# Gathers that add, replaced by gathers into work tiles and separate adds

## The chip, the cores and the metric

The kernel runs on one core of a Trainium2 chip. The metric is the time of one execution on the device in microseconds (us); lower is better. The engines in the profile are PE (TensorE, matrix products; PEld is its weight load), DVE (VectorE), ACT (ScalarE), POOL (GpSimd) and SP (SyncE, which here only issues DMAs). POOL also issues the DMAs whose rows are picked by a list of indices (DMA_INDIRECT). Each engine runs its own instructions strictly in order; semaphores make one engine or DMA wait for another.

## The reference

Sixteen sequences of 256 tokens, 128 values each, in float32, pass two layers. Between the steps every token is normalised.

```
x = x + 0.5 * moe(layernorm(x))            # "a"
x = x + attention(layernorm(x))            # 16 heads of 8, differential, causal
x = x + 0.5 * moe(layernorm(x))            # "b", the same weights
x = x + 0.5 * quant_ffn(layernorm(x))      # "qa"
x = x + linear_attention(layernorm(x))     # "l", a scan over the tokens
x = x + 0.5 * quant_ffn(layernorm(x))      # "qb"
```

The part that the change touches is the mixture of experts, which runs twice. A shared expert serves every token; of eight further experts each token takes the two with the highest router score, weighted by the softmax of these two scores:

```
logits = xf @ router_w.T + experts_bias
rw, sel = jax.lax.top_k(logits, 2)
rw = softmax(rw)
cw = (one_hot(sel, 8) * rw[..., None]).sum(axis=1)
eo = silu(einsum('td,edh->teh', xf, w1)) * einsum('td,edh->teh', xf, w3)
out = einsum('te,teh,ehd->td', cw, eo, w2) + shared_out
```

## The kernel before

The 4096 tokens lie in SBUF all the time, as eight blocks `xs[k]` of 128 partitions x 4 tiles (`NT`) x 128 values; a block is two sequences. Every step updates its block in place.

A mixture is done for a group of one or two blocks (`GROUPS`, line 35): "a" for [0], [1], [2, 3], [4, 5], [6, 7], "b" for [0, 1], [2, 3], [4, 5], [6], [7]. The first, a0, runs every expert over all its tokens. The other nine route:

- `route` (line 550) normalises the blocks, scores the tokens and picks two experts for each; `send` (line 642) computes for each token the two rows (`pos`) that it gets in a table sorted by expert.
- `scatter` (line 695) copies the tokens into that table in DRAM (`slots_x`) by indirect DMAs of 128 rows from POOL, line 714, two in flight at a time.
- `experts` fetches the table in tiles of 128 rows (`xg`), runs each through the weights of its one expert (`wst`, loaded by SP; products `pgu` and `poy` on PE, the gate `hr` on ACT, DVE and sometimes POOL), scales the rows by the token's weight and writes them to a second table in DRAM (`slots_y`), issued by ACT.
- `collect` (line 939) waits for all experts of the group and for the shared expert and then starts one `gather` for each block (line 952).
- `gather` brings each token its two rows. For both of the two choices (`i`) and each of the four tiles (`t`) an indirect DMA from POOL (line 966) reads 128 rows of `slots_y` and adds them to `x[:, t, :]` as it writes. That is eight DMAs a block, and 15 blocks make 120. The second choice's DMA of a tile must come after the first has landed, since both add to the same bytes.

The first reader of the new tokens is `stats` (line 505): for each tile one `bn_stats` and one `bn_aggr` on DVE (lines 512, 513), then on POOL a small addition and a power (lines 516, 500), then on DVE `nm` (line 520). After "a" the attention (`project`, `maxima`, `weights`, `values`, `output`) follows, after "b" `quant` (line 1503), `linear` and `quant` again. The linear stage (`linear_f`, line 1689) runs eight rounds for each block: it loads `kv` (256 KB, line 1693, by SP), multiplies it by the keys (line 1698), scans (line 1701, DVE), multiplies by the queries (line 1705) and adds to a product on PE.

Nothing of this is a fixed loop. Each step is a Python generator that yields what it needs: engines it may run on with a cost, buffers and events. `Order.run` plays all of them against a book of free times for engines and buffers and issues the instructions one by one; so it decides the order on every engine. Two things of that matter here. `sb2` (line 392) offers an elementwise step to DVE or POOL, and the one that would finish first in the book takes it (DVE is charged 1 us extra). And `best_order` (line 306) makes 60 trial plans, each after the first with the ranks of five kinds of task moved at random, draws these from the sorted list of task names, and keeps the plan whose book ends first.

Work tiles are taken by tag from a fixed number of buffers and given back with `done`. Tag `w5` has seven buffers of 128x512 and serves the gates of the shared expert, the quantised layer's `thq`, and the linear stage's `kv`, `state`, `vT` and `thl`, and early on some weights that are unpacked.

Of the kernel before, what the change touches and what calls it, by code (L numbers as in the profile page):

```python
# [15 lines left out]
ALU = mybir.AluOpType  # L16
# [3 lines left out]
P = 128  # L20
B, S, D = 16, 256, 128
NBLK = 8
NT = 4
# [16 lines left out]
def slot_tiles(nt):  # L40


    return (2 * nt * P + E * (P - 1)) // P
# [207 lines left out]
def by_rows(index):  # L251
    return index if isinstance(index, Dry) else bass.IndirectOffsetOnAxis(ap=index, axis=0)
# [37 lines left out]
def e_pool(n, k=1):  # L290
    return k * (0.25 + n * 0.0029)
# [36 lines left out]
def program(order, nc, tc, const, small, work, ps, t_in, out):  # L328
# [40 lines left out]
    def W(tag, shape, name, dtype=F32):  # L369
        return (tag, name, shape, dtype)  # L370
# [13 lines left out]
    def hold(*want):  # L384

        return Op([("", 0.0)], want)
# [5 lines left out]
    def sb2(n, *want, need=None):  # L392

        return Op([("DVE", 0.16 + n * 0.0014), ("POOL", e_pool(n))], want, need)
# [10 lines left out]
    def on(g):  # L405
        return nc.vector if g.eng == "DVE" else nc.gpsimd
# [532 lines left out]
    def collect(w, j, rank):  # L939

        r = R[w, j]
        if (w, j) in DENSE:
            yield Wait(*(f"dense {w}{j}.{e}" for e in range(E)))
        else:
            yield Wait(f"experts {w}{j}", *(f"shared {w}{j}.{n}" for n in range(r["n"])))
            names = [f"gather {w}{j}.{n}" for n in range(r["n"])]
            for n, name in enumerate(names):
                order.add(name, gather(w, j, n), rank, order.events[f"experts {w}{j}"])
            yield Wait(*names)
        order.release(r["index"], 0.0)  # L950

    def gather(w, j, n):

        r = R[w, j]
        nt = NT * r["n"]
        sy = slots_y[w, j % 2][0 : slot_tiles(nt) * P]
        x = xs[GROUPS[w][j][n]]
        if n:
            yield Wait(f"gathering {w}{j}.{n - 1}")
        landed = {}  # L960
        for i in range(2):
            for t in range(NT):
                need = (landed[t],) if i else (order.events[f"experts {w}{j}"],)
                g = yield Op([("POOL", 1.6)], kb=1, need=need)
                a = i * nt + n * NT + t
                nc.gpsimd.indirect_dma_start(  # L966
                    x[:, t, :], None, sy, by_rows(r["pos"][:, a : a + 1]),
                    compute_op=ALU.add,
                )
                landed[t] = g.t  # L970
        order.mark(f"gathering {w}{j}.{n}", 0.0)
        order.mark(f"gathered {w}{j}.{n}", max(landed.values()))


    wqkv, bqkv = ctile([P, 640], "wqkv"), ctile([P, 640], "bqkv")
# [747 lines left out]
    def mixture(w, j, rank, *names):  # L1723
        n = f"{w}{j}"
        order.add(f"route {n}", after(route(w, j, rank), "ident", *names), rank)
        for i, k in enumerate(GROUPS[w][j]):
            order.add(f"shared {n}.{i}", shared(w, j, i, k), rank)
        if (w, j) in DENSE:
            for e in range(E):
                order.add(f"dense {n}.{e}", dense_expert(w, j, e), rank + 0.01 * e)  # L1730
        else:
            order.add(f"experts {n}", experts(w, j, rank), rank)
        order.add(f"collect {n}", after(collect(w, j, rank), f"route {n}"), rank)
# [43 lines left out]
    for j, blocks in enumerate(GROUPS["b"]):  # L1777
        rank = 10.0 - j
# [73 lines left out]
```

## Time and profile before

Three runs took 1311.86, 1313.22 and 1316.47 us; the median is 1313.22 us.

| what | value |
|---|---|
| profiled execution | 1316.87 us |
| its span, first to last instruction | 1315.2 us |
| mean granted clock of TensorE in it | 0.965 |
| DMA traffic | 149.68 MB, 114 GB/s over the span |
| POOL, other large groups: line 500, `rr` (16 powers of 128x32) | 87.9 us |
| line 500, `rs` (40 powers of 128x4) | 46.0 us |
| line 1705 on POOL (33) and on DVE (31) | 47.3 and 28.1 us |
| line 1698 on POOL (28) and on DVE (36) | 42.4 and 27.3 us |
| line 1577 on POOL (12) and on DVE (4) | 16.7 and 3.2 us |
| issue to landing, median: line 714 | 2.9 us |
| issue to landing, median: line 966 | 3.7 us |

The page of the profile gives for each engine its busy time and share of the span. A second part shows the span in 40 equal slices, one digit each (9 is 90% busy or more); PEclk is the clock that the throttle granted TensorE. Groups of instructions are shown as line, engine, operation, output<-inputs and count, then busy time in us and the mean of one in ns, then the idle time of that engine just before them and what ended most of it. "issue" there is time in which the engine waited for nothing that the profile shows. The chain of waits follows the work that ended last back from the last instruction.

The runs of line 966 start at 164, 303, 433, 563, 696, 909, 1033, 1111 and 1169 us.

### The profile page before, as it was taken

Reading aid. Unit: us, or ns where it says so; the run is one execution under the profiler, and the core shown is the slowest. Engines: PE = TensorE matmul, PEld = TensorE weight load, DVE = VectorE, ACT = ScalarE, POOL = GpSimd, SP = SyncE. Lnnn points to the kernel's source line nnn. Section 1 sums busy time; section 2 is a strip of 40 time slices with the busy share of each in tenths; the row PEclk is TensorE's granted clock in tenths of the full one; section 3 lists DMA queues with packets and bytes.
Section 4 is the critical chain, followed back from the end, with each engine's and each line's share of the span. In section 5 each row is a group of like instructions: output and inputs, shape, how many; then the busy total and the mean of one; then the engine's idle time right before and its main releaser. Section 6 shows DMA issues by size and latency. Waiting matters only on the chain. (4 is left out here: it accounts for less than half of the span.)

```text
span 1315.2 us, 32976 instructions
## 1 busy us (share of the span) xinstructions
PE 1175.2 (89%) x12480; PEld 853.7 (65%) x12480; DVE 897.6 (68%) x2059; ACT 655.5 (50%) x1163; POOL 821.7 (62%) x972
## 2 busy tenths in 40 slices
PE   6797889999899979998987799999999869898888
PEld 3465666676576667766754577767567657675566
DVE  5465667776678655594776568768748757587993
ACT  2153456554555544645633475664564524544424
POOL 4213546738862882384458735477867788779874
PEclk9898999999999989998998799999999989998989
DMA  4675563525344335445222333314445766642331
GB/s 127 147 194 132 140 161 87 143 67 125 88 128 128 52 86 159 127 105 125 69 82 27 88 90 104 88 52 110 100 129 161 206 158 169 169 127 77 93 100 33
DMA packets 213006, 149.68 MB, mean 114 GB/s; under 512 B 18544, under 2 KB 200944, under 8 KB 212848
## 3 DMA queue, kind: packets, MB, share of 16 engines
q1 hardware_dynamic: 155376, 113.70, 31.0%
q0 software_dynamic: 21120, 15.81, 6.8%
q10 hardware_dynamic: 36352, 18.07, 4.8%
q8 instruction: 99, 1.62, 0.5%
q14 instruction: 59, 0.48, 0.1%
HBM read 117.32 MB, written 30.19 MB: 112 GB/s over the span
## 5 line engine op out<-in xcount | busy, mean ns | idle before, releaser
L409 PE MATMUL pgu<-xTg,wst 128*128 128x128 f32 x1464 | 218.5, 285 | 10.9 <-DMA wst<-in_w_dram 6.1
L409 PEld LDWEIGHTS pgu<-xTg,wst 128*128 128x128 f32 x1464 | 188.7, 195 | 37.8 <-issue 19.2
L1264 DVE TENSOR_REDUCE qpad<-scores 128x8 f32<-128x2048 f32 x64 | 146.4, 2288 | 40.2 <-PE scores L413 39.7
L1323 ACT ACTIVATE ex<-scores 128x2048 f32<-128x2048 f32 x64 | 120.2, 1878 | 85.6 <-PE scores L413 85.5
L409 PE MATMUL poy<-wst,hr 128*128 128x128 f32 x732 | 117.3, 287 | 20.2 <-POOL hr L754 9.1
L413 PE MATMUL scores<-qm,kT 32*128 32x256 f32 (+1 forms) x2048 | 114.1, 349 | 16.1 <-DVE qpad L1264 9.8
L413 PE MATMUL scores<-kT,qT 32*128 32x512 f32 (+1 forms) x1024 | 113.4, 536 | 14.0 <-ACT ex L1323 4.9
L409 PEld LDWEIGHTS poy<-wst,hr 128*128 128x128 f32 x732 | 98.5, 196 | 36.8 <-DVE hr L737 11.7
L966 POOL DMA_INDIRECT x<-slots_yb,pos x64 | 106.5, 1664 | 17.5 <-issue 15.8
L928 ACT ACTIVATE y<-poy,xg 128x128 f32<-128x128 f32 x162 | 59.2, 368 | 98.0 <-PE poy L409 93.1
L413 PEld LDWEIGHTS scores<-qm,kT 32*128 32x128 f32 x2048 | 79.6, 189 | 41.5 <-DVE qpad L1264 16.2
L413 PE MATMUL pav<-ex,vaug 128*32 128x512 f32 (+1 forms) x1024 | 98.4, 503 | 2.3 <-ACT ex L1323 2.2
L966 POOL DMA_INDIRECT x<-slots_ya,pos x56 | 87.6, 1565 | 17.2 <-issue 14.2
L500 POOL TENSOR_TENSOR rr<-ss,mhalf 128x32 f32<-128x32 f32 x16 | 87.9, 5492 | 16.5 <-DVE ss L1401 16.4
L714 POOL DMA_INDIRECT slots_xa<-xng,pos x56 | 56.0, 1001 | 61.3 <-DMA slots_xa<-xng,pos 30.4
L413 PEld LDWEIGHTS pol<-owr,state 128*128 128x128 f32 x512 | 68.5, 207 | 37.9 <-POOL state L1705 18.9
L413 PE MATMUL pol<-owr,state 128*128 128x128 f32 x512 | 74.8, 295 | 20.3 <-POOL state L1705 13.9
L516 POOL TENSOR_SCALAR rs<-mv 128x4 f32<-128x4 f32 (+1 forms) x56 | 19.8, 353 | 117.2 <-DVE mv L513 116.4
L1701 DVE TENSOR_TENSOR_SCAN state<-lam,kv 128x512 f32<-128x512 f32 x64 | 90.3, 1423 | 1.4 <-POOL kv L1698 1.1
L413 PEld LDWEIGHTS <-shift 32*128 32x128 bf16 x3072 | 59.2, 95 | 48.3 <-issue 37.5
L714 POOL DMA_INDIRECT slots_xb<-xng,pos x64 | 67.6, 1057 | 35.4 <-DMA slots_xb<-xng,pos 13.5
L1247 DVE TENSOR_REDUCE qpad<-scores 128x16 f32<-128x2048 f32 x32 | 73.2, 2289 | 22.7 <-PE scores L413 22.4
(250 smaller groups left out, 2651.8 us busy)
## 6 DMA issues: line engine op xcount, KB each, us to landing
wst<-in_w_dram SPq DMA_DIRECT2D x573, 128.0 KB
kv<-values_l SPq DMA_DIRECT2D x64, 256.0 KB
xg<-slots_xb SPq DMA_DIRECT2D x21, 258.0 KB
slots_yb<-y ACTq DMA_DIRECT2D x21, 256.0 KB
xg<-slots_xa SPq DMA_DIRECT2D x18, 258.0 KB
slots_ya<-y ACTq DMA_DIRECT2D x18, 256.0 KB
slots_xa<-zero ACTq DMA_DIRECT2D x10, 258.0 KB
slots_xb<-zero ACTq DMA_DIRECT2D x10, 258.0 KB
```

The costliest lines, as they stand in the source:

```text
L409: nc.tensor.matmul(dst, lhsT, rhs, start=start, stop=stop)
L413: nc.tensor.matmul(dst, lhsT, rhs, start=start, stop=stop, skip_group_check=True)
L500: nc.gpsimd.tensor_tensor(dst, src, mhalf[:, :n], ALU.pow)
L516: nc.gpsimd.tensor_scalar(rs, mv[:, 0:nt, 1], LN_EPS, None, ALU.add)
L714: ins = nc.gpsimd.indirect_dma_start(sx, by_rows(r["pos"][:, i * nt + t : i * nt + t + 1]), xn[:, t, :], None,)
L928: nc.scalar.activation(y[:, i, :], po[:, 0:D], AF.Copy, scale=xg[:, i, D:SW])
L966: nc.gpsimd.indirect_dma_start(x[:, t, :], None, sy, by_rows(r["pos"][:, a : a + 1]), compute_op=ALU.add,)
L1247: nc.vector.tensor_reduce(qp[:, 0, T0 : T0 + 2, :, :, HD].rearrange("p t m g -> p m t g"), s.rearrange("p m (t g n) -> p m t g n", t=2, g= ...
L1264: nc.vector.tensor_reduce(qp[:, 1, T, :, :, HD], s.rearrange("p m (g n) -> p m g n", g=G), AX.X, ALU.max, negate=True)
L1323: nc.scalar.activation(ex0, s, AF.Exp, scale=1.0 / math.sqrt(HD))
L1701: nc.vector.tensor_tensor_scan(state, lam, kv, 0.0, ALU.mult, ALU.add)
```

## The change

`gather` no longer adds in the DMA. For each of the two choices it takes a work tile `rows` of tag `w5`, fetches the four tiles' rows into it with plain indirect DMAs, and starts a new task `added` that adds the 512 columns of `rows` to the block in one step, on DVE or POOL as `sb2` decides, and gives the work tile back. In the book a fetch costs POOL 1.05 instead of 1.6, and every second one sets `landed`, for which the next two wait (in the book alone: they write to different places). `gathered`, for which the attention or `quant` of the block waits, is now marked when both adds are done. `gather` and `added` take the rank of their mixture.

```diff
@@ collect
-                order.add(name, gather(w, j, n), rank, order.events[f"experts {w}{j}"])
+                order.add(name, gather(w, j, n, rank), rank, order.events[f"experts {w}{j}"])
@@
-    def gather(w, j, n):
+    def added(x, rows):
+        g = yield sb2(NT * D)
+        on(g).tensor_tensor(x, x, rows, ALU.add)
+        g.done(rows)
+
+    def gather(w, j, n, rank):
@@
-        landed = {}
+        landed = order.events[f"experts {w}{j}"]
         for i in range(2):
+            g = yield hold(W("w5", [P, NT, D], "rows"))
+            rows = g[0]
             for t in range(NT):
-                need = (landed[t],) if i else (order.events[f"experts {w}{j}"],)
-                g = yield Op([("POOL", 1.6)], kb=1, need=need)
+
+                g = yield Op([("POOL", 1.05)], kb=1, need=(landed,))
                 a = i * nt + n * NT + t
-                nc.gpsimd.indirect_dma_start(
-                    x[:, t, :], None, sy, by_rows(r["pos"][:, a : a + 1]),
-                    compute_op=ALU.add,
-                )
-                landed[t] = g.t
+                nc.gpsimd.indirect_dma_start(rows[:, t, :], None, sy, by_rows(r["pos"][:, a : a + 1]))
+                if t % 2:
+                    landed = g.t
+            order.add(f"add {w}{j}.{n}.{i}", added(x, rows), rank, g.t)
         order.mark(f"gathering {w}{j}.{n}", 0.0)
-        order.mark(f"gathered {w}{j}.{n}", max(landed.values()))
+        yield Wait(*(f"add {w}{j}.{n}.{i}" for i in range(2)))
+        order.mark(f"gathered {w}{j}.{n}", max(order.events[f"add {w}{j}.{n}.{i}"] for i in range(2)))
```

## The prediction

> **What bounds the kernel now.** I read the share of each engine and the slices first, then TensorE (PE) in stretches with and without gathers, then the gathers on GpSimd (POOL), then the chain of waits.
>
> ```profile
> PE 1175.2 (89%) x12480; PEld 853.7 (65%) x12480; DVE 897.6 (68%) x2059; ACT 655.5 (50%) x1163; POOL 821.7 (62%) x972
> PE   6797889999899979998987799999999869898888
> POOL 4213546738862882384458735477867788779874
> PEclk9898999999999989998998799999999989998989
> ```
>
> TensorE is busy 89% of the span, so 140 us (1315.2 - 1175.2) is all that a better order can win outright. The slices show where it sits: after the first four, every PE digit below 8 stands over a 7 or 8 of POOL. So I cut the span by hand into the eight stretches in which the gathers of line 966 run, and, as a second list, the stretches between them. Columns: length, then busy time of PE, PEld, DVE, ACT and POOL, granted clock, DMA share, GB/s.
>
> ```profile
> 300.00:345.00 45.00, 39.81 (x484) 27.93 (x487) 26.48 (x81) 24.84 (x38) 39.34 (x37) 1.00 0.49 105
> 695.00:745.00 50.00, 34.59 (x471) 20.32 (x471) 28.78 (x53) 17.40 (x22) 42.74 (x50) 0.79 0.32 63
> 905.00:950.00 45.00, 42.79 (x536) 30.84 (x529) 33.02 (x91) 25.77 (x46) 39.15 (x40) 0.96 0.46 97
> sum 355.00, PE 294.11 PEld 216.07 DVE 227.42 ACT 157.06 POOL 301.66; mean PE 36.76 PEld 27.01 DVE 28.43 ACT 19.63 POOL 37.71
> ...
> sum 780.00, PE 738.96 PEld 536.99 DVE 577.39 ACT 431.69 POOL 458.48; mean PE 92.37 PEld 67.12 DVE 72.17 ACT 53.96 POOL 57.31
> ```
>
> With gathers, PE idles 355 - 294.11 = 60.9 us (17.2%), and POOL is busy 85%. Between them PE idles 780 - 738.96 = 41.0 us (5.3%). At the lower rate the gather stretches would idle 0.053 x 355 = 18.7 us, so about 42 us is their excess: the most that the gathers can be charged with. It is uneven: 695 to 745 loses 15.4 us of 50 at a clock of 0.79, 905 to 950 only 2.2 of 45. In the first, two blocks fetch 16 times in a row, the scatters of the next group stand behind them on POOL, and TensorE has only attention left until the next xg lands at 744.
>
> ```profile
> L966 POOL DMA_INDIRECT x<-slots_yb,pos x64 | 106.5, 1664 | 17.5 <-issue 15.8
> L966 POOL DMA_INDIRECT x<-slots_ya,pos x56 | 87.6, 1565 | 17.2 <-issue 14.2
> L714 POOL DMA_INDIRECT slots_xa<-xng,pos x56 | 56.0, 1001 | 61.3 <-DMA slots_xa<-xng,pos 30.4
> L714 POOL DMA_INDIRECT slots_xb<-xng,pos x64 | 67.6, 1057 | 35.4 <-DMA slots_xb<-xng,pos 13.5
> L512 DVE BATCH_NORM_STATS2 st<-x 128x6 f32<-128x128 f32 x192 | 51.3, 267 | 17.6 <-DMA x<-slots_yb,pos 16.1 <-DMA x<-in_x_dram 0.8 <-DMA x<-slots_ya,pos 0.6
> ```
>
> A gather takes 1.6 us of POOL and waits almost only for "issue", 0.3 us: back to back, one starts every 1.86 us. The first reader of the tokens, the statistics of line 512 on VectorE (DVE), already waits 16 us for landings. From the chain of waits:
>
> ```profile
> 1112.60 1.49 POOL x L966
> 1114.09 0.38 issue
> 1114.47 1.80 POOL x L966
> 1116.27 0.48 issue
> 1116.75 1.60 POOL x L966
> 1118.35 0.76 issue
> 1119.11 1.54 POOL x L966
> ```
>
> Between 1054 and 1126, and again at 1184, the chain runs through gathers; after 1190 it runs through DVE and PE (DVE 92.08 busy of 100 from 1190 to 1290), where there are none.
>
> **What the change removes.** 120 gathers that add: 106.5 + 87.6 = 194.1 us busy, and 30.0 us of "issue" before them (the engine's waits for line 966), 224 us of POOL.
>
> **What it adds: 120 plain gathers.** The trace has none. The nearest row is the plain scatter of line 714, through the same queue, 128 rows each: 56.0 + 67.6 = 123.6 us for 120, mean 1.03. From below, its shortest, 0.954 us, gives 114.5; from above, the adding gather's own 194.1 if the add costs POOL nothing. I take 1.03. With 0.30 of issue a gather is started every 1.33 us, and POOL gets back 194.1 - 123.6 = 70 us (bounds 0 and 80).
>
> **30 adds of 128x512** (15 blocks, two each), on DVE or POOL by the order's choice. Of the present 128x512 steps with that choice in the last stage (lines 1698, 1705, 1577) DVE has 36 + 31 + 4 = 71 and POOL 28 + 33 + 12 = 73, so half and half: on DVE 0.76 to 0.91 us by the means of lines 1698 and 1705, 15 x 0.84 = 13 us; on POOL 1.39 to 1.52 by lines 1577 and 1698, 15 x 1.46 = 22 us. POOL ends 48 us lighter, DVE 13 us heavier; DVE is busy only 227 of 355 us in the gather stretches, which hides its part (13 us without that cover).
>
> The GPSIMD Engine Reference, section 4.1 "Engine selection", sends elementwise adds to VectorE and calls GpSimd about twice as slow for two inputs. The trace agrees (0.68 against 1.32 us, medians of line 1698). By that rule all 30 adds would go to DVE, and POOL would win the whole 70 us. The page SBUF — State Buffer, section "SBUF: two separate sides", speaks against the change: a VectorE step with two SBUF inputs and a GpSimd step that reads SBUF lock each other out of a shared port. In the trace line 1698 ranges from 0.66 to 1.75 us on DVE and from 1.25 to 2.19 on POOL, as such a lock would make it. If every add blocked the other engine for its own length, 30 x 1.1 = 33 us would be spread over both, by my estimate.
>
> **The path of a block.** Now eight gathers take 7 x 1.86, the last lands 3.7 us after its start, and one tile of statistics is left (0.27 + 0.18): 17.2 us. A group of two blocks takes 15 x 1.86 + 4.1 = 32.0. After: 7 x 1.33, landing after 2.9 (the scatter's), the second add (1.1, the mean of both engines, and 0.2 to be seen), then all four tiles of statistics, since the add covers the block (4 x 0.45 = 1.8): 15.3 us; for two blocks 15 x 1.33 + 6.0 = 26.0. Nine groups gather, three of one block and six of two: 243.6 us now, and 3 x 1.9 + 6 x 6.0 = 41.7 less after, 17%. An excess idle of 42 us that follows the length of the runs shrinks by 17%: **7 us**. Had a plain gather the adding one's cost, every run would be 2.6 us longer, 24 us or 10% in all, a loss of 4.
>
> **The waits it moves.** An add stands on its engine until four rows have landed. On DVE the maxima (line 1264) and gates (737, 749) queue behind it, and the scores and poy matmuls wait for those; on POOL it is the next gathers, hr (754) and rs (516). It takes the place of the wait of line 512, 16.7 us in all now; I put the difference at 0, between -16 (none is left) and +16 (it doubles).
>
> **The work tiles** come from tag w5, seven buffers, which the linear stage uses for kv and state. SyncE's queue already waits some 87 us for such a buffer before the kv loads (line 1693). From 1032 to 1186 eight row tiles would hold one for 3 x 1.33 + 2.9 + 1.1 = 8 us each, 64 of 7 x 154 = 1078 us, 6%: 0 to 5 us. I take 0, because both engines together wait only 6.4 us for the kv loads themselves, which are early; without that cover, 5 us and every weight load behind it on SyncE.
>
> **Sum.** The profiled execution took 1316.87 us (span 1315.2 and 1.67 around it). Less 7.2 is 1309.7. It lies 3.65 above the median of the runs, 1313.22, so the forecast is **1306 us**; its own range is 1300 (13 us, 31% of 42, if nothing is paid at the runs' ends) to 1309.
>
> **Rivals.** *The pairs lengthen the runs.* The order now lets a pair wait for the landing of the one before (2.0 in its books after 2 x 1.05), where the adding gathers followed each other at once. Nothing on the chip has to wait there, but POOL runs its instructions in the planned order, and whatever is put into the gap delays the next pair. With 2 x 1.33 + 2.0 = 4.66 per pair, eight gathers take 3 x 4.66 + 1.33 + 6.0 = 21.3 us, sixteen 39.9: 3 x 4.1 + 6 x 7.9 = 60 us more, 25% of 42: +10, **1323**. It decides from a mean spacing of about 1.7 us (15 x 1.73 + 6 = 32). For it: POOL has some 108 us of other work in these stretches, about enough to fill the gaps. Against it: that work then comes earlier, and the total is smaller; scatters in pairs repeat every 3.85 us (155.49 to 159.34), at which the loss is only 3 us.
>
> *A new order starves TensorE once more.* Which instruction stands where on every engine comes from a search over 60 trial plans, which draws its moves from the list of task names. "add" tasks lengthen the list, so every draw after the first trial differs and the order changes everywhere. Price: one more stretch like 695 to 745 against an ordinary one, 15.4 - 2.6 = 13 us, **1326**. For it: that stretch differs from 905 to 950, with the same 16 gathers, by 13 us for the order alone. Against it: the same draw may win 13.
>
> *The gathers are hidden anyway.* The excess is attention's own wait (in 695 to 745 TensorE waits by name for DVE's maxima and ACT's exponentials), so **1313**. Against it: the chain between 1054 and 1126.
>
> **How the numbers follow.** Within 0.3% (4 us) is what a measurement of this kernel cannot tell from no change. Forecast 0.45 (faster), hidden 0.12 (same), pairs 0.23 and new order 0.20 (slower, 0.43 together). The range goes down by the forecast's 13 and a lucky order's 13 (1287) and up by both slow rivals (1335).
>
> **What would show it.** Plain gathers of 1.0 to 1.1 us in the groups, POOL busy near 775 us, DVE near 910; mean spacing within a run below 1.6 (right) or above 1.7 (pairs); PE idle in the gather stretches below 60 us; statistics waiting for an add, no longer for a landing; kv loads waiting no more than 90 us for buffers. The prediction is wrong if a plain gather costs POOL 1.5 us, or if PE idles longer in stretches that hold no gathers.

## The result and the profile after

| | runs | median us | lowest to highest |
|---|---|---|---|
| before | 12 | 1312.55 | 1309.67 to 1316.74 |
| after | 12 | 1320.85 | 1312.61 to 1326.92 |

The ratio is 1.0061, 95% interval 1.0045 to 1.0077: the change makes the kernel some 8 us slower. That lies inside the range of the prediction and on the other side of its forecast.

From the page of the changed kernel, the same four lines as before (busy time and share of each engine, then the slices):

```profile
PE 1174.7 (89%) x12480; PEld 851.4 (64%) x12480; DVE 903.6 (68%) x2059; ACT 648.5 (49%) x1150; POOL 797.9 (60%) x1008
PE   6787899999899979999996999998899987998987
POOL 4213547706852880365478733688886568868784
PEclk9899999999899989999997999999999998999888
```

POOL is 24 us lighter, TensorE is as busy as before, and the span (1320.0 us) is longer by 4.8. So TensorE idles 145.3 us, against 140.0. Something in the kernel got 24 us cheaper and the engine that bounds it stood 5 us longer. The groups of the fetches, of the adds and of the first reader of the tokens (busy time, mean ns of one, then the engine's idle time just before them and what ended it):

```profile
L973 POOL DMA_INDIRECT rows<-slots_yb,pos x64 | 71.3, 1114 | 15.1 <-issue 12.5 <-DMA slots_xb<-xng,pos 0.6 <-PE pgu L409 0.3
L973 POOL DMA_INDIRECT rows<-slots_ya,pos x56 | 56.2, 1003 | 25.3 <-issue 24.7 <-DMA slots_xb<-xng,pos 0.3
L954 POOL TENSOR_TENSOR x<-x,rows 128x512 f32<-128x512 f32 x17 | 22.2, 1304 | 16.6 <-DMA rows<-slots_ya,pos 9.6 <-DMA rows<-slots_yb,pos 6.2 <-issue 0.8
L954 DVE TENSOR_TENSOR x<-x,rows 128x512 f32<-128x512 f32 x13 | 10.3, 792 | 14.7 <-DMA rows<-slots_yb,pos 10.7 <-DMA rows<-slots_ya,pos 2.6 <-issue 1.5
L512 DVE BATCH_NORM_STATS2 st<-x 128x6 f32<-128x128 f32 x192 | 51.1, 266 | 24.6 <-POOL x L954 23.8 <-DMA x<-in_x_dram 0.7
```

A fetch costs POOL (71.3 + 56.2) / 120 = 1.06 us instead of 1.62. The adds wait 16.6 + 14.7 us for landings, and the statistics wait 23.8 us more for adds: 55 us in all, where one wait of 17.6 us stood before. How that comes about is seen in the timeline of POOL at the first block that gathers (start, duration, line, operation, in brackets the idle time before it and what ended it):

```profile
162.07 0.98 POOL L973 DMA_INDIRECT rows<-slots_ya,pos  x1 [0.29 <-issue]
163.36 0.95 POOL L973 DMA_INDIRECT rows<-slots_ya,pos  x1 [0.30 <-issue]
164.34 0.26 POOL L516 TENSOR_SCALAR rs<-mv 128x4 f32<-128x4 f32 x1
164.68 1.04 POOL L500 TENSOR_TENSOR rs<-rs,mhalf 128x4 f32<-128x4 f32 x1
165.92 1.08 POOL L973 DMA_INDIRECT rows<-slots_ya,pos  x1 [0.19 <-issue]
...
172.00 1.27 POOL L954 TENSOR_TENSOR x<-x,rows 128x512 f32<-128x512 f32 x1 [2.31 <-DMA rows<-slots_ya,pos]
173.43 1.09 POOL L973 DMA_INDIRECT rows<-slots_ya,pos  x1 [0.17 <-issue]
```

Between pairs the plan has put other steps, and at 172.00 the block's own first add waits 2.3 us for a landing, ahead of the last four fetches. POOL runs in order, so the second half of the block cannot be fetched before the first half is added. Over the nine runs of gathers, the time from first to last start sums to 332 us, where it was 258 before (mean spacing 2.2 to 3.9 us instead of 1.9 to 3.1). The forecast saw these runs shrink; here they grow, with instructions a third shorter.

TensorE in stretches, cut by hand as before (length, busy time of PE, PEld, DVE, ACT, POOL, granted clock, DMA share, GB/s); first those with gathers, then those between:

```profile
693.00:736.00 43.00, 30.58 (x432) 19.57 (x434) 18.23 (x30) 15.83 (x21) 32.58 (x47) 0.80 0.30 84
882.00:942.00 60.00, 51.92 (x635) 35.60 (x634) 54.63 (x99) 30.60 (x53) 53.25 (x53) 1.00 0.42 120
sum 387.00, PE 331.61 PEld 240.25 DVE 267.23 ACT 178.21 POOL 308.05; mean PE 36.85 PEld 26.69 DVE 29.69 ACT 19.80 POOL 34.23
...
1208.00:1308.00 100.00, 82.44 (x417) 57.19 (x417) 79.21 (x132) 36.77 (x71) 75.54 (x77) 0.86 0.23 69
sum 761.00, PE 712.09 PEld 519.10 DVE 544.78 ACT 409.01 POOL 432.52; mean PE 79.12 PEld 57.68 DVE 60.53 ACT 45.45 POOL 48.06
```

The last stretch of the kernel before that holds no gathers, as long as the one from 1208 above:

```profile
1190.00:1290.00 100.00, 88.39 (x483) 63.84 (x483) 92.08 (x131) 42.05 (x80) 83.19 (x78) 0.92 0.26 80
```

With gathers PE idles 55.4 us (60.9 before), between them 48.9 (41.0 before). The 100 us after the last run alone, in which no gather runs (1208 to 1308, before 1190 to 1290), idle 17.6 us instead of 11.6; taken to the end of the span it is 21.7 instead of 16.9. No fetch runs there, so this part is put down to another order of the same work.

### The profile page after: what moved, and what is told of

It reads as the page before. It is cut to its first block, busy times and chain, and to the rows that moved or that the text cites. A ratio compares the mean times of both kernels' runs of the same rounds, so it can differ in the third digit from the quotient of the medians.

```text
span 1320.0 us, 33068 instructions
## 1 busy us (share of the span) xinstructions
PE 1174.7 (89%) x12480; PEld 851.4 (64%) x12480; DVE 903.6 (68%) x2059; ACT 648.5 (49%) x1150; POOL 797.9 (60%) x1008
## 3 DMA queue, kind: packets, MB, share of 16 engines
q8 instruction: 99, 1.62, 0.5%
## 4 chain that ended last, share of the span: by engine, by line
PE 52%; POOL 15%; DVE 14%; DMA 9%; issue 5%; ACT 4%; SPq 0%; POOLq 0%; ACTq 0%; DVEq 0%
PE scores L413 13%; PE pgu L409 8%; PE pav L413 5%; DVE qpad L1271 4%; PE poy L409 4%; POOL rows L973 3%; PE pg L409 3%; PE poq L409 2%; ACT ex L1330 2%; DMA rows<-slots_yb,pos 2%; PE pu L409 2%; PE phq L409 2%; DMA wst<-in_w_dram 2%; DMA slots_xa<-xng,pos 2%; DVE state L1708 2%
## 5 line engine op out<-in xcount | busy, mean ns | idle before, releaser
L409 PE MATMUL pgu<-xTg,wst 128*128 128x128 f32 x1464 | 213.8, 283 | 19.2 <-DMA wst<-in_w_dram 9.0
L413 PE MATMUL scores<-qm,kT 32*128 32x256 f32 (+1 forms) x2048 | 112.4, 345 | 19.5 <-DVE qpad L1271 11.6
L409 PE MATMUL poy<-wst,hr 128*128 128x128 f32 x732 | 114.6, 284 | 10.0 <-POOL hr L754 4.6
L928 ACT ACTIVATE y<-poy,xg 128x128 f32<-128x128 f32 x170 | 62.2, 369 | 98.6 <-PE poy L409 93.4
L749 DVE SCALAR_TENSOR_TENSOR hr<-thr,pgu 128x256 f32<-128x256 f32 x128 | 52.3, 415 | 68.5 <-ACT thr L740 66.5
L500 POOL TENSOR_TENSOR rr<-ss,mhalf 128x32 f32<-128x32 f32 x16 | 87.7, 5479 | 14.7 <-DVE ss L1408 14.5
L1708 DVE TENSOR_TENSOR_SCAN state<-lam,kv 128x512 f32<-128x512 f32 x64 | 87.6, 1381 | 3.5 <-POOL kv L1705 2.9
L714 POOL DMA_INDIRECT slots_xb<-xng,pos x64 | 66.6, 1041 | 37.2 <-DMA slots_xb<-xng,pos 14.2
L413 PE MATMUL pol<-owr,state 128*128 128x128 f32 x512 | 73.0, 290 | 15.2 <-POOL state L1712 11.6
L1254 DVE TENSOR_REDUCE qpad<-scores 128x16 f32<-128x2048 f32 x32 | 73.3, 2289 | 19.1 <-PE scores L413 18.9
L740 ACT ACTIVATE thr<-pgu 128x256 f32<-128x256 f32 x128 | 49.0, 384 | 64.2 <-PE pgu L409 61.9
```

The source lines that it names most:

```text
L409: nc.tensor.matmul(dst, lhsT, rhs, start=start, stop=stop)
L413: nc.tensor.matmul(dst, lhsT, rhs, start=start, stop=stop, skip_group_check=True)
L500: nc.gpsimd.tensor_tensor(dst, src, mhalf[:, :n], ALU.pow)
L714: ins = nc.gpsimd.indirect_dma_start(sx, by_rows(r["pos"][:, i * nt + t : i * nt + t + 1]), xn[:, t, :], None,)
L740: nc.scalar.activation(th, pg, AF.Tanh, scale=0.5)
L749: nc.vector.scalar_tensor_tensor(h, th, 1.0, pg, ALU.add, ALU.mult)
```

## The experiments

Two things changed at once: the instructions of the gathers, and through the list of task names and the new costs the order of everything. The first aim was to part them. Expectations name theories in capitals; by FETCH they mean that plain fetches in quick succession do harm by themselves, by ADDS that the separate adds come too late, by ORDER that the redrawn plan is what costs. All ratios are against the kernel before on the same chip, with the 95% interval; the five groups of runs were on five chips.

### First group: instructions and order parted

e1 keeps the old order and its book exactly and only swaps instructions: plain fetches into idle memory, and one add of 512 columns on DVE as soon as the book reaches the landing. 13 of the 15 blocks are done so (104 fetches, 26 adds); the two blocks of b1 keep their 16 adding gathers.

```diff
-                nc.gpsimd.indirect_dma_start(x[:, t, :], None, sy, by_rows(...), compute_op=ALU.add)
+                nc.gpsimd.indirect_dma_start(rows[i][:, t, :], None, sy, by_rows(...))
...
+            order.late.append((max(landed.values()), x, rows[i]))
@@ Order.issue
+            if eng == "DVE":
+                for item in [x for x in self.late if x[0] <= s]:
+                    self.late.remove(item)
+                    self.vector.tensor_tensor(item[1], item[1], item[2], ALU.add)
```

> The order of the kernel before on every engine, but 104 of the 120 gathers (all but group b1) are plain fetches into tiles whose memory is idle then, and each of the 26 adds stands on VectorE directly ahead of the first instruction that the old plan starts after the landing. The exchange of instructions without a new order. Theory ORDER (the loss of 8 us comes from the newly drawn order, the exchange itself gains): 1302 to 1311, so 2 to 10 us below before. Theory EXCHANGE (waiting for the landing and adding cost more than the shorter gathers give): 1317 or more.

e2 is the reverse: the order of the changed kernel, with gathers that add.

```diff
@@ added
-        on(g).tensor_tensor(x, x, rows, ALU.add)
@@ gather
-                nc.gpsimd.indirect_dma_start(rows[:, t, :], None, sy, by_rows(...))
+                nc.gpsimd.indirect_dma_start(x[:, t, :], None, sy, by_rows(...), compute_op=ALU.add)
```

> The order of the changed kernel, but with gathers that add and without the 30 adds (their places in the plan stay empty). Theory ORDER: as slow as the changed kernel or slower, 1320 to 1332, since the longer gathers now stand in the poor order. Theory EXCHANGE: back to 1313 or below.

e3 and e4 take the search away from the kernel before and from the changed one, so that both run on unmoved ranks:

```diff
@@ best_order
-    return Order(moved)
+    return Order({})
```

> The kernel before with the default ranks, no search over plans. The book of the plan ends at 1348 instead of 1314. Theory ORDER: clearly slower than before, by 10 to 35 us (1323 to 1348), as the book says. If the book says nothing of the chip: within 5 us of 1313.

> The changed kernel with the default ranks, no search. The book ends at 1343, 5 less than for the kernel before with default ranks. Theory ORDER: slower than the changed kernel but not slower than e3 (0 to 15 us below it). Theory EXCHANGE: slower than e3 by 5 us or more.

Measured: e1 1.0399 [1.0353, 1.0444], e2 1.0149 [1.0107, 1.0191], e3 1.0038 [1.0010, 1.0067], e4 1.0348 [1.0309, 1.0386]. Both kernels with plain fetches are slower by 3.5 to 4%, those with adding gathers by 0.4 and 1.5%. (e3 missed the 10 to 35 us expected of ORDER: its book ends 34 later and it ran 4 us slower.) But on this chip the kernel before itself took 1346 us, 34 more than the median above. In e1 TensorE stood still 43.3 us with no cause that the profile names, against under 1 us in the same kernel on another chip (e9, below). PE, then POOL, around the first run of fetches in e1 (timeline, columns as above):

```profile
167.06 0.66 PE L552 MATMUL ptg<-ident,xg 128*128 128x128 f32 x4
174.55 2.09 PE L421 MATMUL scores<-kT,qT 32*128 32x512 f32 x8 [6.83 <-issue]
```

```profile
166.85 0.98 POOL L983 DMA_INDIRECT rows<-slots_ya,pos  x1 [5.68 <-DMA slots_ya<-y]
168.14 0.95 POOL L983 DMA_INDIRECT rows<-slots_ya,pos  x1 [0.30 <-issue]
...
174.40 0.94 POOL L983 DMA_INDIRECT rows<-slots_ya,pos  x1 [0.30 <-issue]
```

TensorE starts nothing for 6.83 us, from the first of eight fetches to the second last. All four of its stands of this kind above 2 us in e1 lie within such bursts. That made FETCH the leading theory for the second group. Such stands turned out to belong to this chip, so e1 to e4 are left out of the sums below; e3 and e4 weren't run again.

### Second group: bursts, adds, and another draw

e5 is the changed kernel again, as it is.

> The changed kernel itself, beside the kernel before on the chip of this group. If chips differ in how they treat the plain fetches (in e1 and e4 TensorE stood up to 6.8 us for nothing that the profile names, in the first profile of the change never over 0.5): a ratio above 1.010 here, with such stands in the profile. If they do not: 1.0045 to 1.0077 as before.

e6 is e1 with five small memsets after each plain fetch, which give POOL's saving back and space the fetches as adding gathers are:

```diff
+                    for _ in range(5):
+                        nc.gpsimd.memset(spacer, 0.0)
```

> e1 with five small memsets (0.12 us each) on GpSimd after each plain fetch, so that fetches start about every 1.8 us, as the adding ones do, instead of every 1.3. Theory FETCH (several plain fetches in flight hold up the loading of TensorE's own instructions, which shows as waits for nothing, 43 us in e1): these waits fall below 10 us and the ratio from 1.040 to 1.000 to 1.010, although GpSimd is no less busy than before. Theory ADDS (the 26 adds on VectorE cost it): stays above 1.025.

e7 is e1 without the line that issues the adds: the rows fetched for 13 blocks are never added to the tokens. The fetches and all else stay.

```diff
-                    self.vector.tensor_tensor(item[1], item[1], item[2], ALU.add)
```

> e1 without its 26 adds: the fetched rows of 13 blocks are never added to the tokens. Theory FETCH: within 1% of e1's ratio (1.030 to 1.045), waits for nothing on TensorE still above 30 us. Theory ADDS: 1.000 to 1.010.

e8 is the kernel before with another seed of its search, nothing else:

```diff
-    rng = random.Random(3)
+    rng = random.Random(7)
```

> The kernel before with another start of the random draws (7 instead of 3), nothing else. The book of its plan ends at 1306 instead of 1314. Theory ORDER: a ratio that differs from 1 by 0.5% or more in either direction (the book says 0.994). If the order drawn matters little: 0.997 to 1.003.

Measured: e5 1.0083 [1.0051, 1.0115], e6 1.0113 [1.0085, 1.0140], e7 0.9797 [0.9751, 0.9842], e8 0.9970 [0.9953, 0.9987]. FETCH falls: e7 has all fast fetches and is 2% faster than before, and e6, where they are spaced, is slower. ADDS does not fit either: both results lie outside what the two theories expected. The groups of e6:

```profile
L983 POOL DMA_INDIRECT rows<-slots_ya,pos x56 | 55.7, 994 | 12.9 <-issue 3.3 <-DMA slots_ya<-y 3.2
L985 POOL MEMSET spacer<- 128x1 f32 x520 | 53.1, 102 | 24.1
...
L240 DVE TENSOR_TENSOR x<-x,rows 128x512 f32<-128x512 f32 x26 | 18.7, 721 | 44.5 <-DMA rows<-slots_ya,pos 24.6 <-DMA rows<-slots_yb,pos 15.2 <-issue 4.5
```

The 520 memsets take back 53.1 us of POOL, about what 104 fetches save (104 x 0.56 = 58). The runs of gathers are then 263 us long, as before the change (258), and the adds wait 39.8 us for landings. So, where POOL's gain is given back and the rows land as late as before, the exchange costs 1.1%.

### Third group: the same instructions and orders again, and the pairs

e9 is e1, e10 is e2, on another chip. e11 is the changed kernel with seed 6, and e12 the changed kernel without the pairs:

```diff
@@ e12, gather
-                if t % 2:
-                    landed = g.t
```

> e1 once more, since its chip was 34 us slower for every kernel and showed the waits for nothing on TensorE. e7 (the same without the adds) had 0.980. Theory ADDS (26 adds that stand at the head of VectorE's queue until the landing take back what the shorter gathers give): 1.005 to 1.020, so 25 to 40 points of a thousand above e7, with few waits for nothing. Theory FETCH (back-to-back plain fetches hold up TensorE's instructions on every chip): 1.03 to 1.045 with waits for nothing above 30 us.

> e2 once more: the order of the changed kernel with gathers that add and without the adds. The changed kernel has 1.006 to 1.008. Theory ORDER: 1.008 or more. Theory EXCHANGE (fetch and add cost more than the adding gather, in one and the same order): 1.003 or less.

> The changed kernel with another start of the random draws (6); the book of its plan ends at 1314, as that of the kernel before does, instead of 1329. Theory ORDER: 0.990 to 1.002. Theory EXCHANGE: 1.005 or more, as with the first draw.

> The changed kernel without the pairs: every fetch needs only the experts' end in the book, so that the eight of a block follow each other. The order is drawn anew (book 1317). Theory PAIRS (the gaps between pairs lengthen the runs from 17 to 20 us and from 32 to 40 to 57, which is the loss): runs of eight in 11 to 14 us and a ratio of 0.990 to 1.002. If the pairs are not to blame: 1.005 or more. Waits for nothing on TensorE above 10 us would show why they are there.

Measured: e9 **0.9774** [0.9746, 0.9802] (1279.68 us, the fastest of all), e10 1.0263 [1.0232, 1.0294], e11 0.9926 [0.9901, 0.9951], e12 1.0105 [1.0075, 1.0134]. First e9, the old order with plain fetches: its page, then its groups, then its stretches with gathers and, in the last line, those between.

```profile
PE 1155.3 (91%) x12480; PEld 838.7 (66%) x12480; DVE 912.6 (72%) x2085; ACT 654.7 (51%) x1163; POOL 763.7 (60%) x972
```

```profile
L983 POOL DMA_INDIRECT rows<-slots_ya,pos x56 | 54.2, 968 | 18.2 <-issue 16.2 <-DMA slots_ya<-y 1.6 <-DMA xg<-slots_xb 0.2
L240 DVE TENSOR_TENSOR x<-x,rows 128x512 f32<-128x512 f32 x26 | 18.7, 719 | 9.7 <-DMA rows<-slots_yb,pos 4.2 <-issue 2.8 <-DMA rows<-slots_ya,pos 2.6
L520 DVE BATCH_NORM_STATS2 st<-x 128x6 f32<-128x128 f32 x192 | 51.1, 266 | 1.6 <-DMA x<-in_x_dram 1.4
```

```profile
672.00:698.00 26.00, 18.29 (x268) 11.19 (x260) 17.28 (x27) 9.61 (x10) 21.11 (x26) 0.88 0.15 44
881.00:921.00 40.00, 36.32 (x463) 25.88 (x465) 28.09 (x83) 23.43 (x42) 35.14 (x34) 1.00 0.50 107
sum 252.00, PE 225.36 PEld 165.13 DVE 187.37 ACT 123.59 POOL 201.30; mean PE 25.04 PEld 18.35 DVE 20.82 ACT 13.73 POOL 22.37
...
sum 867.00, PE 806.49 PEld 586.94 DVE 633.90 ACT 472.77 POOL 505.27; mean PE 89.61 PEld 65.22 DVE 70.43 ACT 52.53 POOL 56.14
```

e9 is faster than both theories had expected. POOL is 821.7 - 763.7 = 58 us lighter, just the saving of 104 fetches, and the runs of gathers are 209 us long instead of 258. The adds wait 9.7 us instead of e6's 44.5. In the stretches with gathers, shorter now, PE idles 252 - 225.36 = 26.6 us, where it was 60.9; between them 60.5, where it was 46.3 (41.0 to 1290 and 5.3 from there to the end, since e9's list runs to the end of its span). Over the whole span it idles 120.5 us instead of 140.0 and is itself busy 19.9 us less, at a mean clock of 0.981 instead of 0.965. e7, with no adds at all, has nearly the same ratio on another chip (0.9797): in this order the 26 adds cost nothing that could be measured.

The opposite corner, e10, is the new order with adding gathers (page and groups):

```profile
PE 1181.6 (88%) x12480; PEld 856.5 (64%) x12480; DVE 907.7 (67%) x2046; ACT 647.9 (48%) x1150; POOL 846.7 (63%) x991
```

```profile
L972 POOL DMA_INDIRECT x<-slots_yb,pos x64 | 109.3, 1707 | 15.3 <-issue 14.3 <-PE phq L409 0.3 <-DVE nm L520 0.2
L512 DVE BATCH_NORM_STATS2 st<-x 128x6 f32<-128x128 f32 x192 | 51.4, 268 | 17.1 <-DMA x<-slots_yb,pos 16.0 <-DMA x<-in_x_dram 0.9
```

The span is 1347.3 us, TensorE idles 165.7, and the runs of gathers sum to 363 us. So it is the new order that lengthens the runs, from 258 to 363; the exchange shortens them again, to the 332 of the change. The four corners, as ratios to the kernel before:

| | gathers that add | plain fetches, adds | exchange alone |
|---|---|---|---|
| old order | 1 | 0.9774 (e9) | -2.3% |
| new order | 1.0263 (e10) | 1.0061 (the change) | -2.0% |
| new order alone | +2.6% | +2.9% | |

**The exchange wins 2.0 to 2.3%, 26 to 30 us, in either order; the new order loses 2.6 to 2.9%, 34 to 38 us.** Together they make the measured +0.6%. (The two exchanges are not quite one edit: e9's covers 13 of 15 blocks and adds on DVE alone, the change's covers all and adds on both. Each difference in the table is uncertain by 0.3 to 0.4.)

As for the pairs: without them (e12) the runs shrink from 332 to 289 us in all, and the kernel is no faster, 1.0105. With another draw and the pairs kept (e11) they last 340 us and the kernel is 0.7% faster than before. The length of these runs does not decide which order is good. But e12 has a newly drawn order too, and the next group shows how much a draw can do, so this one run does not measure the pairs.

### Fourth group: is the loss of the order luck?

e13 is the kernel before and e14 the changed one with seed 16; e15 and e16 are e1's exchange in the book of the kernel before with the seeds 7 and 16, so that each has its adding twin (e8, e13) with the same moves.

> The kernel before with a third start of the draws (16), whose plan the book ends at 1337 instead of 1314. Theory LUCK (the 2.6% that the order of the change costs in e10 is the draw's): 1.005 to 1.025, a spread among draws of one kernel as wide as that loss. Theory STRUCTURE (the new costs and waits in the book make worse orders, whatever is drawn): 0.995 to 1.005, as e8.

> The changed kernel with a third start of the draws (16; book 1328, against 1329 and 1314 for the draws that gave 1.007 and 0.993). LUCK: anywhere from 0.985 to 1.020. STRUCTURE: 0.990 or more, that is never near the 0.977 of e9.

> e9's exchange (104 plain fetches, 26 adds on VectorE that the book does not know) in the order of e8's draw, 7. STRUCTURE: 0.970 to 0.982, since any order planned with the old entries gains the 2.2% of e9. LUCK: the gain of the exchange is the same in every order, e8's 0.997 less 2.2%: also 0.970 to 0.982; a value above 0.990 would mean that e9's gain belongs to one order.

> The same exchange in the order of draw 16, that of e13. Both theories: 0.015 to 0.030 below e13. If e13 is slow and this is slow too, by the same, order and exchange add up.

Measured: e13 1.0233 [1.0207, 1.0259], e14 1.0074 [1.0047, 1.0100], e15 0.9801 [0.9784, 0.9819], e16 1.0074 [1.0054, 1.0093]. So one seed changes the untouched kernel by 2.3%, nearly as much as the new order costs. And in the two other orders the exchange wins 0.9970 to 0.9801, 1.7% (on two chips), and 1.0233 to 1.0074, 1.6%.

### Fifth group: a longer search

e17 and e18 take the best of 1200 trial plans instead of 60, for the changed kernel and for e1's exchange in the old book, with its moves written into the kernel, and are otherwise as they were.

```diff
-    return Order(moved)
+    return Order({"l 0 2": 0.326, "shared a4": 0.965, "route a1": -1.905,
...
+    })
```

> The changed kernel in the best order of 1200 plans instead of 60, another start; its book ends at 1304 instead of 1329. The three draws so far took 6 to 11 us less than their books (1320.6 to 1329, 1302.8 to 1314, 1320 to 1328, on the scale of a kernel before of 1312.6). Theory ORDER: 1293 to 1300 on that scale, a ratio of 0.985 to 0.990. If the book says nothing below 1314: 0.993 or more.

> e9's exchange in the best order of 1200 plans for the kernel before; its book ends at 1305 instead of 1314. The book of draw 7 ended at 1306 and gave 0.980 (e15). Expected 0.970 to 0.982; below 0.975 it would be the fastest version here.

Measured: e17 0.9853 [0.9822, 0.9885] (1288.34 us), e18 0.9850 [0.9821, 0.9879]. The changed kernel with a longer search beats the kernel before by 1.5%. e18 missed what was expected of it, and e9 with its 60 plans stays the fastest. The plan's own book (where the planner's sums end, not a time of the chip) against the ratio measured:

| kernel | book's end | ratio |
|---|---|---|
| before, e8 / as it is / e13 | 1306 / 1314 / 1337 | 0.997 / 1 / 1.0233 |
| changed, e17 / e11 / e14 / as it is | 1304 / 1314 / 1328 / 1329 | 0.9853 / 0.9926 / 1.0074 / 1.0061 |

Within each kernel a book that ends later goes with a slower run, but for the last two of the change, whose books differ by 1. Two kernels outside the table do not fit: e12, whose book ends at 1317, had 1.0105, and e3, at 1348, had 1.0038 on the first group's chip. The book is blind to the exchange, though: for e1's kernel it ends at 1314 in e9 and at 1305 in e18, which is the slower of the two.

Over 16 other starts of 60 plans each (seeds 0 to 16 without 3), the book ended at 1322.1 on average for the kernel before and at 1324.8 for the changed one, with single starts between 1306 and 1337. The search of the kernel before had drawn 1314.3, 8 better than its average, and the changed one 1329.3, 5 worse than its own. By the book, then, some 12 of the 15 by which the plans differ are the draw, and the other 3 are not clear of the scatter. On the chip this split wasn't made: the seeds tell that a draw alone can move 2.3%, not how much of the 2.6 to 2.9% is the draw and how much the pairs, the new costs and the tasks for the adds. That e17 and e18 come out level speaks for a small part of the latter; but over the four draws of each the changed kernel averages 0.998 and e1's exchange in the old book 0.987, with 2 to 3 points between the draws of either. So the split stays open.

## Why the prediction was wrong in sign

**Plain gathers of 1.03 us, from the scatter's row: right** (1.06). The adds were right too: 17 on POOL and 13 on DVE, 1.30 and 0.79 us for 1.46 and 0.84. The rule that the prediction quoted (the Trainium skill, GPSIMD Engine Reference, section 4.1 "Engine selection") holds again in these two rows (POOL takes 1.6 times as long), and in e9, where all 26 adds go to DVE, POOL keeps the whole saving. DVE, forecast near 910, was busy 903.6. Of the 33 us that the adds might cost by blocking the other engine nothing is seen in e9, which is as fast with its 26 adds as e7 is without.

**POOL near 775 us: 797.9.** The exchange itself gives 821.7 - 66.6 + 22.2 = 777.3. The other 20.6 us are elementwise steps that the new plan gives to POOL: it runs 36 instructions more, of which the adds are 17. This is the first place where the order shows.

**"The path of a block", 7 us for a run that is 17% shorter: the mechanism right, the size wrong.** In the fixed order (e9) the runs shrink by 258 - 209 = 49 us; the same step of the prediction, 0.53 us less a fetch between 1.86 and 1.33, gives 51 for the 13 blocks. So the shortening was right, and what a shorter run is worth was not: the share of excess idle, 42 x 17%, gave 7 us, and the runs showed 19.5 us less idle and 19.9 us less busy time of TensorE, together 39 in the profiled executions and 30 between the medians. Two things were missing. The excess idle is not in proportion to the length: at the rate of the stretches between (60.5 / 867, 7.0%) the 252 us would idle 17.6, so e9's excess is 9 us where it was 42, and of the 34.3 us that the stretches with gathers idle less, 14 came back between them. And in e9 the idle time avoided came with a higher granted clock and shorter matmuls, which the sum left out: the stretch 693 to 736 of the changed kernel idles 12.4 of 43 us at 0.80, the same place in e9 7.7 of 26 at 0.88. (The idle share is the same, 29 and 30%, so the share alone does not set the clock.)

**The step that failed is the one that took the order as kept.** The forecast costed each edit in the old plan, and put the redraw aside as a rival, "13 us" from one pair of stretches, with the remark that the same draw may win as much. With the instructions held fixed the redrawn order cost 34 to 38 us (e10 against the kernel before, the change against e9). A difference between two stretches of one plan is no measure of how far two plans lie apart; the seeds show 2.6% between the best and the worst of three draws of the kernel before.

**Waits that the change moves, put at 0 with 16 either way: 37 us more** (55 against 17.6). In e9 they shrink (9.7 us before the adds, and 1.6 before the statistics, almost all of it for the first load), and in e10, the new order without adds, the statistics wait 17.1, as before. So they come neither with the adds nor with the new order alone, but with the places that the new plan gives the adds. They cannot have cost much: the exchange wins 2.0% in the new order with them, and 2.3% in the old one without. What they cost by themselves was not measured.

**Work tiles from w5, put at 0: nearly right.** The kv loads on SP wait some 98 us for buffers, against 94 counted in the same way before (the prediction had counted 87); 8 us of it is for rows and the adds. DVE and POOL wait 12.4 us for the kv loads instead of 6.4, but as long, 12.1, in e10, where no rows are fetched into those tiles: this too comes with the order.

**The rivals.** *The pairs lengthen the runs* passed its own test, a spacing above 1.7 us, but the runs last longer than it said, since POOL's other work fills them (332 us, where 3 x (21.3 - 6.0) + 6 x (39.9 - 6.0) = 249 would follow from its lengths). That the pairs are the cause is not borne out: e11 and e17 keep them, with runs of 340 and 348 us, and are faster than the kernel before, and e12 without them is no faster than the change. Since every one of these is another draw, a part of the pairs in the loss is not excluded. *A new order starves TensorE once more* is what happened, mis-sized and in other places: the stretch 693 to 736 is no worse than it was, and 5 to 6 us more idle after 1208. *Hidden* is refuted by e9. Of the signs named, "PE idle in the gather stretches below 60" came true (55.4), and so did the one against: PE idles longer where there are no gathers (48.9 against 41.0).

## What to carry to other kernels

When a program plans its own order, an edit changes two things, and a seed of its search can be worth more than the edit. Compare edits with the order held fixed, and orders with the instructions held fixed; judge a redraw by several draws of the untouched kernel. An operation on a queue that has other work behind it is worth what it delays: in the old order, 58 us less of POOL made the kernel 30 us faster. How much of this is idle time avoided and how much shorter matmuls differs from run to run, as the next section shows.

## What was not expected of the hardware

**A fetch without the add moves the same bytes in far fewer packets.** The queue that POOL fills is a line of its own in the list of queues (packets, MB, share of the 16 engines); the changed kernel's:

```profile
q0 software_dynamic: 7680, 15.81, 4.2%
```

and that of the kernel before:

```profile
q0 software_dynamic: 21120, 15.81, 6.8%
```

A fetch lands after 2.7 us at the median, an adding gather after 3.7.

**Idle time and clock.** TensorE idles 120.5 us and is busy 1155.3 in e9 (clock 0.981), 121.7 and 1152.0 in e15 (0.989), 140.0 and 1175.2 before (0.965), 165.7 and 1181.6 in e10 (0.961). The same 12480 matmuls take 20 us less where 20 us of idle are avoided, and only 6 more where 26 are added. No fixed price follows: e17 idles 119.1 us and is busy 1166.1 (0.979), 9 us less for 21 avoided, and e13 idles 168.9 and is busy 1173.3 (0.963), 2 us less with 29 added. In e7, e9, e15, e17 and e18, with 18 to 22 us less idle than before, the matmuls took 0.4 to 1.3 us less for each us of it. The Trainium skill, TensorE: Matmul & The Clock Gate, section "What's actually happening", says that the clock is throttled by default and that activity releases it; the rows above agree in direction.

**One chip stands apart.** The same kernel, e1 and e9, was 1.0399 there and 0.9774 on another chip. On it TensorE stood without a named cause for 43.3 us in e1 and 18.9 in e4, both with plain fetches, and for less in the kernels with adding gathers (6.8 in e2, 2.3 in e3); in e9, e12 and e5 on other chips it was under 1 us, and on the fourth group's chip at most 4.5 (e16; 3.9 in e13, which has adding gathers). What that chip does during bursts of plain fetches wasn't settled.
